# Fused four-layer residual kernel on one core: gathers placed behind a step's fourth maximum, three queries normed inside the attention loop, and smaller moves

## The chip, the core and the metric

The kernel runs on one core of a Trainium2 chip. The core has five engines that run their own instruction streams side by side: TensorE (PE, matrix products and transposes; its weight loads appear as PEld), VectorE (DVE), ScalarE (ACT), GpSimd (POOL) and SyncE (SP, which here only starts DMA transfers). The metric is the device time of one execution in microseconds, lower is better. The time of a kernel is the median of its runs.

## The reference

The input `x` is 64 sequences of 64 tokens with 512 features, float32. Four layers each add to it:

```
x = x + (x @ W[id] + b[id])                    # one of 16 experts for each sequence
x = x + (x @ W1.T + scaling * (x @ A.T) @ Bm.T)# one of 8 adapters of rank 16
x = x + attention(x)
x = x + (weights[subject] over the 64 tokens + bias[subject])   # one of 8 subjects
```

The attention has 8 query heads in 4 groups of keys and values, 64 wide. Queries and keys are normalised, multiplied by a gain and rotated by their position. The new keys and values are written into a paged cache of blocks of 16 positions, and each sequence then attends to the 256 positions up to each token:

```
q = rope(rms(q) * (1 + q_scale), pos)
k = rope(rms(k) * (1 + k_scale), pos)
k_blocks, v_blocks = cache with k, v written at pos
scores = q . k / 16, masked to pos - 256 < kpos <= pos
out = softmax(scores) . v @ Wo.T
```

## The kernel before

**Tiles and order.** The 4096 tokens are 32 tiles (`NT`) of 128, two sequences each. The order of instructions on every engine is the order in which the program writes them: a queue of its own for each engine, no reordering. The engines meet through semaphores. Scratch tiles come from pools; a tile's next use waits until the last reader of its buffer is done. PSUM has eight banks: seven in a ring that nearly all products share (`bank`, L99), and one, `py`, in a pool of its own (`pyp`).

**First part** (L185 to L784). The expert products (`layer0`, L275), their transposes (`turn0`, L298 and the addition at L299), and the adapter layer (`layer1`, L650 to L665) run over groups of 1, 1, 2 and then 4 tiles. Between them lie the transposes of the layer's result (`turn_x2`, L684), the product with the weights of keys and values and that with the weights of queries (`product`, L140, named `pk` and `pq`), and the normalisation and rotation of both (`turned`, L116 to L135). In `turned` ACT squares (L120), DVE sums (L122), ACT takes the root (L123), DVE forms the reciprocal (L126) and multiplies (L128), two more multiplications by half rows (L133) and one by a whole row (L134) rotate, and an addition on engine `X` (L135) ends it. Keys and values of all tiles go to `kvd` in memory (`keep_kv`), where old cache rows are copied as well (`copies`, L155 on POOL and L161 on SP). DVE also works out tables of addresses (`windows`, for example L498) and the sines and cosines (`rotation`). Near the start `warm` (L222) runs three and then six matmuls of the identity with itself, whose results nobody reads.

**Late queries.** With `LATE = 8`, the queries of tiles 25 to 31 are not made in the first part. Those of 25 to 30 are made in a loop ahead of the attention (L995 to L1003): product, `parts_q`, and two tiles later `turn_q` (L170), which transposes the query (`pqt`), lets ACT copy it twice and writes it to memory as `qTd`, from where `load_q` fetches it two steps before its use. Tile 31 has its product in step 0 of the loop, in the bank `py`; its normalisation runs in steps 0 to 3, so the bank is held until L128 of step 2 has read it. `turn_q` of tiles 29, 30 and 31 runs in steps 0, 4 and 5.

**Attention loop** (L1008 to L1046). Step `s` runs in this order:

1. `load_kv(s + 2)`: five gathers (L801) on POOL, by addresses that DVE worked out; masks, queries (SP).
2. `scores(s)`: eight products `ps` (L874); for each, DVE adds the mask and finds the maximum in one instruction (L882), ACT forms the exponential and its sum (L886).
3. POOL's addition to `w3` (`add_one`, L847); `load_pair`.
4. `attend(s - 1)`: 48 small matmuls `po` (L921, L934), then two copies to `oT` on DVE (L939).
5. `normalise(s)`: reciprocals and eight multiplications on DVE (L894, L898).
6. in even steps `last(s - 4)`: `pz` (L961), the fourth layer of two tiles.
7. `project(s - 2)`: `py` (L949) with the output weights, and an addition on DVE (L953).
8. `keys(s + 1)`: transposes `pkt` (L855, L861) and three ACT copies to `kT`.
9. `turn(s)`: transposes `ppt` of the normalised scores (L907, L911), copied to `pT` by DVE and ACT in turn (L908), the last by ACT (L912).

The buffers of gathered rows, `kv`, are four (L792). In steps 0 and 1 a POOL copy of one element of `kT` (`after_keys`, L809) stands ahead of the gathers; from step 2 on they only wait for a free `kv` buffer, that is for `po` of an earlier step.

Of the kernel before, what the change touches and what calls it, by code (L numbers as in the profile page):

```python
# [49 lines left out]
LATE = 8  # L50
# [9 lines left out]
def body(ctx: ExitStack, tc: tile.TileContext, a: dict, out: bass.AP):  # L60
# [55 lines left out]
    def turned(ps, n, to, pool, X, kind, cg, sg):  # L116
# [14 lines left out]
        for f in range(2):  # L131
            fs, of = slice(f * HALF, (f + 1) * HALF), slice((1 - f) * HALF, (2 - f) * HALF)
            V.tensor_tensor(t2[:, :, fs], qn[:, :, of], bc(sg[:, None, fs], [128, n, HALF]), ALU.mult)  # L133
        V.tensor_tensor(qn, qn, bc(cg[:, None, :], [128, n, HD]), ALU.mult)  # L134
# [8 lines left out]
    def parts_q(i, pq, X, cs=None):  # L143
        qr = late.tile([128, H, HD], F32, name="qr", bufs=2)
        qrs[i] = qr.rearrange("p h d -> p (h d)")
        return turned(pq, H, qr, late, X, 0, *(cs or gains(0, i, late, X)))
# [23 lines left out]
    def turn_q(i, pool=late):  # L170
# [4 lines left out]
        qT = pool.tile([128, 2, 2, 2, T], F32, name="qTs", bufs=2 if pool is late else 4)  # L175
# [9 lines left out]
    with ExitStack() as pa:  # L185
# [32 lines left out]
        def warm(n):  # L218

            pw = bank("pw")  # L220
            for _ in range(n):
                TE.matmul(pw[:, :128], ident, ident, start=True, stop=True)  # L222

        toki = ptok[:, : 4 * B].rearrange("p (k b) -> p k b", k=4)

        warm(3)
# [7 lines left out]
        warm(6)  # L234
# [497 lines left out]
        for g in range(NG - 1):  # L732
# [9 lines left out]
            for k in range(m):  # L742
# [13 lines left out]
                pk = product(i, wkv, "pk") if half else None  # L756
# [8 lines left out]
                if half == halves - 1:  # L765
                    keep_kv(i, pk if half else product(i, wkv, "pk"), P)
                    if i < NT - LATE:
                        asked.append(i)
                    if len(made) > 1:
                        turn_q(made.pop(0))  # L770
# [24 lines left out]
    kvs, kTs, mbs, prs, pTs, oTs, qTs, pairs, x3s = {}, {}, {}, {}, {}, {}, {}, {}, {}  # L795
# [10 lines left out]
    def after_keys(i):  # L806

        seen = bp.tile([1, 1], F32, name="seen")
        P.tensor_copy(seen, kTs[i][0:1, 0, 0:1])  # L809
# [54 lines left out]
    def scores(i):  # L864
        kT, mb, qT = kTs.pop(i), mbs.pop(i), qTs.pop(i)
        pr = bp.tile([128, G, 2 * NPOS], F32, name="pr")
        mx = bp.tile([128, G, 2], F32, name="mx")
        sm = bp.tile([128, G, 2], F32, name="sm")
        for gp in range(2):
            for b2 in range(2):  # L870
# [8 lines left out]
                for g2 in range(2):  # L879
# [4 lines left out]
                        op0=ALU.add, op1=ALU.min, accum_out=mx[:, g, b2 : b2 + 1],  # L884
                    )
                    S.activation(  # L886
                        p, p, AF.Exp, bias=mx[:, g, b2 : b2 + 1], scale=-1.0, accum_out=sm[:, g, b2 : b2 + 1],
# [26 lines left out]
    def attend(i):  # L914
# [19 lines left out]
        for gp in range(2):  # L934
            for b2 in range(2):
                for g in (2 * gp, 2 * gp + 1):
                    product(b2, g, slice(b2 * 64, (b2 + 1) * 64), 4, G, g, False, gp == 1)
        for b2 in range(2):
            V.tensor_copy(oT[:, :, b2, :], po[b2][:, :256].rearrange("p (k t) -> p k t", t=T))  # L939
# [49 lines left out]
    for i in range(2):  # L989
# [3 lines left out]

    parts = {}
    for i in range(NT - LATE + 1, NT - 1):  # L995
        pq = product(i, wq, "pq")
        parts[i] = parts_q(i, pq, V, cs[i])
# [5 lines left out]
        next(parts[i])  # L1003
    keys(0)
    load_q(1)
    load_mask(1)
    wo = bp.tile([128, KC, D], F32, name="wo", bufs=1)
    for s in range(NT):  # L1008
        if s + 2 < NT:
            if s < 2:  # L1010
                after_keys(s)
            load_kv(s + 2)
# [3 lines left out]
        scores(s)  # L1016
        if s >= 2:
            add_one(s - 2)
        if s:
            load_pair(s - 1)  # L1020
            attend(s - 1)
        else:

            parts[NT - 1] = parts_q(NT - 1, product(NT - 1, wq, "pq", pyp), V, cs[NT - 1])
            turn_q(NT - 3, bp)
        if s == 2:
            next(parts[NT - 1])
        normalise(s, 0)
        normalise(s, 1)
        if s % 2 == 0 and s >= 4:  # L1030
# [5 lines left out]
        if s in (4, 5):  # L1036
            turn_q(NT - 6 + s, bp)
        elif s in (2, 3):

            run(parts.pop(NT - 4 + s))  # L1040
# [4 lines left out]
        elif s == 1:  # L1045
            next(parts[NT - 1])  # L1046
# [5 lines left out]
    attend(i)  # L1052
# [57 lines left out]
```

## Time and profile before

| | us |
|---|---|
| median of 3 runs | 969.09 (968.87 to 969.17) |
| the profiled execution | 969.89 |
| its span | 967.9 |
| mean granted clock of PE in it | 0.993 |

The span is the time from the first to the last record of the profile; the profiled execution's own time lies 2.0 us above it. The attention loop begins with the first `ps` at 542.46 and takes the last 425 us.

The costliest groups of the lines that the change touches (columns: line, engine, operation, output and inputs, shape, count; busy us in all and mean ns of one; idle us of the engine just before them and what ended most of that):

```profile
L801 POOL DMA_INDIRECT kv<-kvd,idxn x128 | 126.5, 988 | 212.8 <-PE po L921 155.8
L886 ACT ACTIVATE pr<-pr,mx 128x320 f32<-128x320 f32 x256 | 140.1, 550 | 7.2 <-DVE mx L882 3.2
L882 DVE CUSTOM_DVE_ANT_0 pr<-ps,mb 128x320 f32<-128x320 f32 x256 | 107.8, 485 | 6.2 <-PE ps L874 4.4
L140 PE MATMUL pq<-wq,x 128*128 128x512 f32 x248 | 111.3, 593 | 0.0
L874 PE MATMUL ps<-kT,qT 64*128 64x320 f32 x512 | 87.3, 460 | 10.8 <-DVE pT L908 6.8
L908 DVE COPY pT<-ppt 128x512 f32<-128x512 f32 x64 | 41.9, 687 | 74.3 <-PE ppt L907 36.4
```

A float32 matmul shows as several records, so 256 products `ps` are 512 records. The gathers (L801) have a third of all of POOL's busy time, and 155.8 us of POOL's idle time before them ended with `po`, that is with the buffer coming free.

### The profile page before, as it was taken

To read this page: it belongs to the slowest core of one execution; us is meant where nothing else is said; L and a number is where in the kernel's file an instruction comes from. 1 tells how busy PE (TensorE), PEld (TensorE's weight loads), DVE (VectorE), ACT (ScalarE), POOL (GpSimd) and SP (SyncE) were. 2 spreads that over 40 slices of the span, in tenths; PEclk is the share of its full clock that TensorE was granted. 3 is DMA by queue.
4 is the path that set the end of the run, shared out by engine and by line. 5 is a ranking of instruction groups with operands and counts; after the bars stand their busy time and mean duration, and the time that the engine had idled before them with its cause. 6 is when DMAs were issued, how large, how long until landed. Compare 5 with 4: busy or idle time off the path is not lost.

```text
span 967.9 us, 17834 instructions
## 1 busy us (share of the span) xinstructions
PE 937.1 (97%) x5425; PEld 513.4 (53%) x5425; DVE 609.0 (63%) x1734; ACT 405.0 (42%) x1081; POOL 402.6 (42%) x604
## 2 busy tenths in 40 slices
PE   8989999999999999999899979999999999999998
PEld 4434444444444444443344546766666666666665
DVE  4744776866976476442216868666767776667673
ACT  1312122322223222233223656656666666666663
POOL 4234355554553544534425543334444333334400
PEclk9989999999999999999999989999999999999999
DMA  8888999999999999999954774766666565666621
GB/s 303 301 291 293 397 397 332 374 375 367 381 335 389 401 339 385 354 362 380 350 217 142 237 254 135 213 206 204 205 197 194 182 193 180 201 197 201 200 68 45
DMA packets 132944, 260.74 MB, mean 269 GB/s; under 512 B 32481, under 2 KB 41186, under 8 KB 132850
## 3 DMA queue, kind: packets, MB, share of 16 engines
q1 hardware_dynamic: 108722, 178.74, 51.3%
q0 software_dynamic: 23232, 79.71, 24.8%
q10 hardware_dynamic: 896, 1.16, 0.3%
q8 instruction: 43, 0.70, 0.3%
q14 instruction: 51, 0.42, 0.1%
HBM read 190.06 MB, written 69.50 MB: 268 GB/s over the span
## 4 chain that ended last, share of the span: by engine, by line
PE 90%; DMA 4%; DVE 3%; SPq 1%; issue 1%; ACT 1%; DVEq 0%; ACTq 0%
PE py L949 12%; PE p L665 11%; PE pq L140 11%; PE p L275 10%; PE pk L140 10%; PE po L921 8%; PE ps L874 8%; PE ppt L907 6%; DMA w<-in_W 3%; PE pkt L855 2%; PE ppt L911 2%; PE px L684 1%; PE pkt L861 1%; PE pqt L174 1%; PE pz L961 1%; PE pt L298 1%
## 5 line engine op out<-in xcount | busy, mean ns | idle before, releaser
L801 POOL DMA_INDIRECT kv<-kvd,idxn x128 | 126.5, 988 | 212.8 <-PE po L921 155.8
L886 ACT ACTIVATE pr<-pr,mx 128x320 f32<-128x320 f32 x256 | 140.1, 550 | 7.2 <-DVE mx L882 3.2
L275 PE MATMUL p<-w,xt 128*64 128x512 f32 x512 | 120.4, 601 | 2.7 <-DMA w<-in_W 2.7
L949 PE MATMUL py<-wo,oT 128*128 128x512 f32 (+1 forms) x264 | 118.3, 591 | 1.7 <-DVE qn L128 1.7
L155 POOL DMA_INDIRECT st<-in_kvc,cidx x68 | 65.9, 970 | 125.1 <-DMA kvd<-st 107.8
L140 PE MATMUL pk<-wkv,x 128*128 128x512 f32 x256 | 115.6, 596 | 0.6 <-ACT x L686 0.6
L665 PE MATMUL p<-w,x 128*128 128x512 f32 x256 | 114.4, 603 | 0.0
L882 DVE CUSTOM_DVE_ANT_0 pr<-ps,mb 128x320 f32<-128x320 f32 x256 | 107.8, 485 | 6.2 <-PE ps L874 4.4
L140 PE MATMUL pq<-wq,x 128*128 128x512 f32 x248 | 111.3, 593 | 0.0
L874 PE MATMUL ps<-kT,qT 64*128 64x320 f32 x512 | 87.3, 460 | 10.8 <-DVE pT L908 6.8
L908 DVE COPY pT<-ppt 128x512 f32<-128x512 f32 x64 | 41.9, 687 | 74.3 <-PE ppt L907 36.4
L133 DVE TENSOR_TENSOR sq<-qn,sg 128x256 f32<-128x256 f32 (+1 forms) x128 | 40.1, 354 | 75.4 <-POOL sg L110 73.5
L898 DVE TENSOR_SCALAR pr<-pr,sm 128x320 f32<-128x320 f32 x256 | 85.2, 394 | 2.2
L921 PE MATMUL po<-pT,kv 128*64 128x128 f32 (+1 forms) x1536 | 84.3, 281 | 1.3 <-issue 1.3
L921 PEld LDWEIGHTS po<-pT,kv 128*64 128x64 f32 (+1 forms) x1536 | 70.5, 137 | 22.0 <-DVE mx L882 14.0
L123 ACT ACTIVATE ss<-ss,epst 128x4 f32<-128x4 f32 (+1 forms) x64 | 19.1, 299 | 146.7 <-DVE ss L122 136.5
L949 PEld LDWEIGHTS py<-wo,oT 128*128 128x128 f32 x264 | 47.5, 189 | 61.5 <-issue 58.4
L665 PEld LDWEIGHTS p<-w,x 128*128 128x128 f32 x256 | 48.3, 193 | 59.0 <-issue 57.2
L140 PEld LDWEIGHTS pk<-wkv,x 128*128 128x128 f32 x256 | 46.3, 190 | 51.1 <-issue 49.8
L275 PEld LDWEIGHTS p<-w,xt 128*64 128x64 f32 x512 | 35.3, 137 | 71.5 <-issue 64.8
L135 POOL TENSOR_TENSOR qr<-qn,sq 128x512 f32<-128x512 f32 x25 | 31.8, 1273 | 90.2 <-DVE qn L134 60.8
L140 PEld LDWEIGHTS pq<-wq,x 128*128 128x128 f32 x248 | 44.9, 190 | 46.2 <-issue 46.2
(202 smaller groups left out, 1336.5 us busy)
## 6 DMA issues: line engine op xcount, KB each, us to landing
w<-in_W SPq DMA_DIRECT2D x62, 1024.0 KB
kvd<-st SPq DMA_DIRECT2D x68, 512.0 KB
xt<-in_xT SPq DMA_DIRECT2D x32, 256.0 KB
x2d<-x2n SPq DMA_DIRECT2D x32, 256.0 KB
kvd<-kvn SPq DMA_DIRECT2D x32, 256.0 KB
qTd<-qTs SPq DMA_DIRECT2D x32, 256.0 KB
qT<-qTd SPq DMA_DIRECT2D x32, 256.0 KB
x2r<-x2d SPq DMA_DIRECT2D x32, 256.0 KB
```

Of the source, the lines that this page charges most:

```text
L140: TE.matmul(ps, x2s[i][:, c, :], w[:, c, :], start=c == 0, stop=c == KC - 1)
L155: P.indirect_dma_start(out=st, out_offset=None, in_=a["kvc"].rearrange("(n r) d -> n (r d)", r=2), in_offset=bass.IndirectOffsetOnAxis(ap= ...
L275: TE.matmul(p0[hs, :], xs[i][:, c, hs], w0s[i][h][:, c, :], start=c == 0, stop=c == KC - 1)
L665: TE.matmul(p1[i], x1s[i][:, c, :], w1[:, c, :], start=c == 0, stop=False)
L801: P.indirect_dma_start(out=kv[:, n, :], out_offset=None, in_=kvd, in_offset=bass.IndirectOffsetOnAxis(ap=at, axis=0),)
L874: TE.matmul(ps[g2][:, :NPOS], qT[rows, gp, b2].rearrange("p h t -> p (h t)"), kT[rows, gp, b2 * NPOS : (b2 + 1) * NPOS], start=True, stop= ...
L882: V.tensor_tensor_reduce(out=p, in0=ps[g2][:, :NPOS], in1=mb[:, b2, :], scale=-1.0, scalar=3.0e38, op0=ALU.add, op1=ALU.min, accum_out=mx[ ...
L886: S.activation(p, p, AF.Exp, bias=mx[:, g, b2 : b2 + 1], scale=-1.0, accum_out=sm[:, g, b2 : b2 + 1],)
L898: V.tensor_scalar(p, p, sm[:, g, b2 : b2 + 1], None, ALU.mult)
L907: TE.transpose(pt[:, n * 128 : (n + 1) * 128], pr[:, g, at : at + 128], ident)
L921: TE.matmul(po[b2][g2 * 64 : (g2 + 1) * 64, gp * 128 : (gp + 1) * 128], kv[rows, n, (G + g) * HD : (G + g + 1) * HD], pT[rows, c, m * 128 ...
L949: TE.matmul(py[:, fs], oT[:, c].rearrange("p b t -> p (b t)"), wo[:, c, fs], start=c == 0, stop=c == KC - 1,)
```

## The change

It has six parts.

1. `warm` and its nine matmuls go.
2. In the first part the last `pk` of a group is written behind `turn0` instead of ahead of it, in groups whose tiles are handled by halves.
3. `turned` and `parts_q` take an engine `M` for the multiplications of the rotation; tile 28 has them, and the addition, on POOL. The buffers of `qTs` outside `late` go from four to three.
4. The tile of maxima, `mx`, becomes two, `mx0` for groups of heads 0 and 1 and `mx1` for 2 and 3. `after_keys` is replaced by `after_scores`: from step 1 on POOL copies one element that the fourth L882 of the step has written, and the five gathers of `load_kv(s + 2)` stand behind this copy, in all steps. Three `load_kv` instead of two run ahead of the loop.
5. `attend` ends without its two `oT` copies; they are `keep_outputs`, behind `normalise`.
6. The queries of tiles 29 to 31 (`LAST` on) are made in another way. The product is copied by ACT into an SBUF tile `raw` (29 ahead of the loop, 30 and 31 in steps 0 and 1 out of the bank `py`). POOL squares them in steps 2 to 4, DVE sums in steps 3 to 5, and in step 6 ACT takes one root for all three, with a one-column exponential behind it, and DVE one reciprocal. POOL multiplies and rotates in steps 7 to 12, two steps for each (`rotate_raw`), and `turn_q` runs in steps 9, 11 and 13. `turn_q` of tile 28 moves into step 1, that of 27 and `keys(0)` change places around the product of 29.

```diff
-    def turned(ps, n, to, pool, X, kind, cg, sg):
+    def turned(ps, n, to, pool, X, kind, cg, sg, M=V):
...
-            V.tensor_tensor(t2[:, :, fs], qn[:, :, of], bc(sg[:, None, fs], [128, n, HALF]), ALU.mult)
-        V.tensor_tensor(qn, qn, bc(cg[:, None, :], [128, n, HD]), ALU.mult)
+            M.tensor_tensor(t2[:, :, fs], qn[:, :, of], bc(sg[:, None, fs], [128, n, HALF]), ALU.mult)
+        M.tensor_tensor(qn, qn, bc(cg[:, None, :], [128, n, HD]), ALU.mult)
...
-        warm(3)
...
-        warm(6)
...
-                pk = product(i, wkv, "pk") if half else None
+                pk = product(i, wkv, "pk") if half and k < m - 1 else None
                 turn0(i0)
...
-                    keep_kv(i, pk if half else product(i, wkv, "pk"), P)
+                    keep_kv(i, pk if half and k < m - 1 else product(i, wkv, "pk"), P)
...
-    def after_keys(i):
+    def after_scores(i):
 
         seen = bp.tile([1, 1], F32, name="seen")
-        P.tensor_copy(seen, kTs[i][0:1, 0, 0:1])
+        P.tensor_copy(seen, mxs[i][0][0:1, 1, 1:2])
...
-        mx = bp.tile([128, G, 2], F32, name="mx")
+        mxs[i] = [bp.tile([128, 2, 2], F32, name=f"mx{gp}") for gp in range(2)]
...
+        return oT, po
+
+    def keep_outputs(oT, po):
         for b2 in range(2):
             V.tensor_copy(oT[:, :, b2, :], po[b2][:, :256].rearrange("p (k t) -> p k t", t=T))
...
-    for i in range(2):
+    for i in range(3):
         load_kv(i)
...
+    def keep_raw(i, pq):
+        S.copy(raw[:, i - LAST].rearrange("p h d -> p (h d)"), pq)
+
+    def rotate_raw(i, part):
+        x, t2, (cg, sg) = raw[:, i - LAST], sqr[:, (i - LAST) % 2], cs[i]
+        if part == 0:
+            P.tensor_tensor(x, x, bc(ssr[:, i - LAST, :, None], [128, H, HD]), ALU.mult)
+            for f in range(2):
+                fs, of = slice(f * HALF, (f + 1) * HALF), slice((1 - f) * HALF, (2 - f) * HALF)
+                P.tensor_tensor(t2[:, :, fs], x[:, :, of], bc(sg[:, None, fs], [128, H, HALF]), ALU.mult)
+        else:
+            P.tensor_tensor(x, x, bc(cg[:, None, :], [128, H, HD]), ALU.mult)
+            P.tensor_tensor(x, x, t2, ALU.add)
+            qrs[i] = x.rearrange("p h d -> p (h d)")
+
     parts = {}
-    for i in range(NT - LATE + 1, NT - 1):
-        pq = product(i, wq, "pq")
-        parts[i] = parts_q(i, pq, V, cs[i])
+    for i in range(NT - LATE + 1, LAST):
+        X = P if i == LAST - 1 else V
+        parts[i] = parts_q(i, product(i, wq, "pq"), X, cs[i], X)
...
+    run(parts.pop(LAST - 1))
     keys(0)
+    keep_raw(LAST, product(LAST, wq, "pq"))
+    turn_q(LAST - 2, bp)
...
     for s in range(NT):
         if s + 2 < NT:
-            if s < 2:
-                after_keys(s)
-            load_kv(s + 2)
             load_mask(s + 2)
...
         scores(s)
+        if s and s + 2 < NT:
+            after_scores(s)
+            load_kv(s + 2)
         if s >= 2:
             add_one(s - 2)
+        if 2 <= s <= 4:
+
+            x = raw[:, s - 2]
+            P.tensor_tensor(sqr[:, s % 2], x, x, ALU.mult)
+        elif 7 <= s <= 12:
+            rotate_raw(LAST + (s - 7) // 2, (s - 7) % 2)
         if s:
             load_pair(s - 1)
-            attend(s - 1)
-        else:
-
-            parts[NT - 1] = parts_q(NT - 1, product(NT - 1, wq, "pq", pyp), V, cs[NT - 1])
-            turn_q(NT - 3, bp)
-        if s == 2:
-            next(parts[NT - 1])
+            outs = attend(s - 1)
+        if s < 2:
+
+            keep_raw(LAST + 1 + s, product(LAST + 1 + s, wq, "pq", pyp))
+        elif s == 6:
+            S.activation(ssr, ssr, AF.Sqrt, bias=epst, scale=1.0 / HD)
+
+            S.activation(ssr1, ssr[:, 0, :1], AF.Exp, scale=-1.0)
         normalise(s, 0)
         normalise(s, 1)
+        if s:
+            keep_outputs(*outs)
+        if s == 6:
+            V.reciprocal(ssr, ssr)
...
-        if s in (4, 5):
-            turn_q(NT - 6 + s, bp)
-        elif s in (2, 3):
-
-            run(parts.pop(NT - 4 + s))
+        if s == 1:
+            turn_q(LAST - 1, bp)
+        elif s in (9, 11, 13):
+            turn_q(LAST + (s - 9) // 2, bp)
+        elif 3 <= s <= 5:
+
+            V.tensor_reduce(ssr[:, s - 3], sqr[:, (s - 3) % 2], AX.X, ALU.add)
         turn(s)
...
-    attend(i)
+    keep_outputs(*attend(i))
```

More of the change, by code (lines that the diff above doesn't have):

```diff
@@ L141, in product, with parts_q @@
         return ps
-    def parts_q(i, pq, X, cs=None):
+    def parts_q(i, pq, X, cs=None, M=V):
         qr = late.tile([128, H, HD], F32, name="qr", bufs=2)
         qrs[i] = qr.rearrange("p h d -> p (h d)")
-        return turned(pq, H, qr, late, X, 0, *(cs or gains(0, i, late, X)))
+        return turned(pq, H, qr, late, X, 0, *(cs or gains(0, i, late, X)), M)
     def copies(to, pool, ahead):
@@ L174, in turn_q @@
             TE.transpose(pqt[:, c * 128 : (c + 1) * 128], qrf[:, c * 128 : (c + 1) * 128], ident)
-        qT = pool.tile([128, 2, 2, 2, T], F32, name="qTs", bufs=2 if pool is late else 4)
+        qT = pool.tile([128, 2, 2, 2, T], F32, name="qTs", bufs=2 if pool is late else 3)
         for gp in range(2):
@@ L216, in body @@
             )
[L218 to L222, printed above, removed]
         toki = ptok[:, : 4 * B].rearrange("p (k b) -> p k b", k=4)
-        warm(3)
         takes = su.tile([E, B], F32, name="takes")
@@ L793, in body @@
     bp = ctx.enter_context(tc.tile_pool(name="bp", bufs=2))
-    kvs, kTs, mbs, prs, pTs, oTs, qTs, pairs, x3s = {}, {}, {}, {}, {}, {}, {}, {}, {}
+    kvs, kTs, mbs, prs, mxs, pTs, oTs, qTs, pairs, x3s = {}, {}, {}, {}, {}, {}, {}, {}, {}, {}
     def load_kv(i):
@@ L883, in scores @@
                         out=p, in0=ps[g2][:, :NPOS], in1=mb[:, b2, :], scale=-1.0, scalar=3.0e38,
-                        op0=ALU.add, op1=ALU.min, accum_out=mx[:, g, b2 : b2 + 1],
+                        op0=ALU.add, op1=ALU.min, accum_out=mxs[i][gp][:, g2, b2 : b2 + 1],
                     )
                     S.activation(
-                        p, p, AF.Exp, bias=mx[:, g, b2 : b2 + 1], scale=-1.0, accum_out=sm[:, g, b2 : b2 + 1],
+                        p, p, AF.Exp, bias=mxs[i][gp][:, g2, b2 : b2 + 1], scale=-1.0, accum_out=sm[:, g, b2 : b2 + 1],
                     )
@@ L992, in body @@
     load_mask(0)
+    LAST = NT - 3
+    raw = bp.tile([128, 3, H, HD], F32, name="raw", bufs=1)
+    sqr = bp.tile([128, 2, H, HD], F32, name="sqr", bufs=1)
+    ssr = bp.tile([128, 3, H], F32, name="ssr", bufs=1)
+    ssr1 = bp.tile([128, 1], F32, name="ssr1", bufs=1)
+    def keep_raw(i, pq):
[11 more added lines that the diff above has]
+            qrs[i] = x.rearrange("p h d -> p (h d)")
     parts = {}
-    for i in range(NT - LATE + 1, NT - 1):
-        pq = product(i, wq, "pq")
-        parts[i] = parts_q(i, pq, V, cs[i])
+    for i in range(NT - LATE + 1, LAST):
+        X = P if i == LAST - 1 else V
+        parts[i] = parts_q(i, product(i, wq, "pq"), X, cs[i], X)
         next(parts[i])
@@ L1044, in body @@
             nc.sync.dma_start(wo, a["woT"].rearrange("(c p) f -> p c f", p=128))
-        elif s == 1:
-            next(parts[NT - 1])
     i = NT - 1
```

## The prediction

> **What bounds the kernel now.** I read the page's busy times and chain first, then busy time by stretch, then the timeline where a stretch shows idle time on PE.
>
> ```profile
> PE 937.1 (97%) x5425; PEld 513.4 (53%) x5425; DVE 609.0 (63%) x1734; ACT 405.0 (42%) x1081; POOL 402.6 (42%) x604
> ...
> PE 90%; DMA 4%; DVE 3%; SPq 1%; issue 1%; ACT 1%; DVEq 0%; ACTq 0%
> ```
>
> PE is the path. The change moves PE's work and removes only nine small matmuls, so all it can win is time in which PE idles or runs slowly: 967.9 - 937.1 = 30.8 us of idle, and slow stretches. Busy time by stretch (second number: PE busy; PEclk is the granted clock):
>
> ```profile
> 52.00:62.65 10.65, 7.08 (x27) 3.66 (x26) 8.69 (x30) 1.05 (x3) 5.20 (x12) 0.68 1.01 366
> 530.00:580.00 50.00, 43.36 (x266) 26.89 (x265) 37.11 (x114) 30.63 (x84) 23.77 (x27) 0.93 0.77 247
> 580.00:930.00 350.00, 341.54 (x2909) 232.69 (x2909) 246.07 (x852) 219.26 (x630) 138.86 (x161) 1.00 0.60 189
> ```
>
> The change touches two of these: the start of the attention loop (530 to 580), and the steady loop, where 350 - 341.54 = 8.46 us are idle. PE in the start of the loop (start, duration, last bracket: idle before it and what ended it):
>
> ```profile
> 517.25 10.46 PE L140 MATMUL pq<-wq,x 128*128 128x512 f32 x24
> ...
> 542.46 3.25 PE L874 MATMUL ps<-kT,qT 64*128 64x320 f32 x16 [1.17 <-issue]
> ...
> 568.09 3.55 PE L874 MATMUL ps<-kT,qT 64*128 64x320 f32 x8 [2.12 <-ACT pT L908]
> 571.57 4.05 PE L921 MATMUL po<-pT,kv 128*64 128x128 f32 x48
> 577.29 3.70 PE L949 MATMUL py<-wo,oT 128*128 128x512 f32 x8 [1.68 <-DVE qn L128]
> ...
> 586.55 2.56 PE L921 MATMUL po<-pT,kv 128*64 128x128 f32 x48
> ```
>
> After 2.12 us of waiting, 48 matmuls of `po` take 4.05 us; in the next step they take 2.56 us. That is half clock: 50 us at 0.93 lack 3.5 us, so about 7 us ran at half. Now a steady step with gathers, and one near the end without:
>
> ```profile
> 824.33 1.91 PE L907 MATMUL ppt<-ident,pr 128*128 128x128 f32 x16
> 825.26 0.95 POOL L801 DMA_INDIRECT kv<-kvd,idxh  x1 [0.30 <-issue]
> 827.41 1.29 DVE L908 COPY pT<-ppt 128x512 f32<-128x512 f32 x2 [3.28 <-PE ps L874]
> 828.16 1.95 PE L874 MATMUL ps<-kT,qT 64*128 64x320 f32 x12 [0.74 <-DVE pT L908]
> ...
> 926.30 1.91 PE L907 MATMUL ppt<-ident,pr 128*128 128x128 f32 x16
> 926.94 0.69 DVE L908 COPY pT<-ppt 128x512 f32<-128x512 f32 x1 [0.84 <-PE ppt L907]
> ```
>
> Without gathers DVE copies the first transposed scores 0.64 us after PE starts them. With gathers it waits 3.08 us, though PE has long gone on. The copy starts 2.15 us after the step's fifth gather (825.26). In the other half of the steps, which hold `pz` and are 0.86 us longer, the fifth gather comes sooner (838.09, 0.07 us after `ppt` at 838.02) and the copy again starts 1.94 us after it (840.03). I read this so: PE's completions reach other engines late while GpSimd writes a gather, until about 2 us after the last one. In steps without `pz` it costs PE 0.74 us here, because `ps` waits for a bank that the copy frees.
>
> **The change part by part.**
>
> *Start of the loop.* PE's work from 517.25 to the first `py` of L949 at 577.29 is, at undisturbed rates: seven products of 3.44, five `pqt` of 0.44, three `pkt` of 1.09, two `ppt` of 2.19, three `ps` of 2.35, two `po` of 2.50: 24.1 + 2.2 + 3.3 + 4.4 + 7.1 + 5.0 = 46.1 us. It took 60.0, so 13.9 are lost: about 6.8 in idle gaps (1.17, 2.12, 1.68 and smaller), 3.5 by the clock, the rest in matmuls that start late. The causes: in step 2 ACT squares a query and loads two tables (3.5 us from 568.41), DVE reduces, and `py` waits until DVE has read the last query out of the single bank (1.68); and ten gathers from 551.77 to 566.3 lie over `ps`, `po` and `ppt`. The change takes the first two away (one ACT copy of 0.60 frees the bank), puts one product behind `ps` of step 1, and lets no gather start in step 1 before its fourth maximum. What it leaves: the softmax of step 0 is covered by one product and `pkt` only. From the start of `ps`: 1.1 us to a table load, 1.28 for it, eight exponentials of 0.545, 1.7 for half a normalisation make some 8.5 us, against 2.35 + 3.44 + 1.09 + half a `ppt`: 8.0; and now fifteen gathers instead of ten run in a row from 523.5 (1.25 us apart: to about 543), over `ps` of step 0 at about 537. Where gathers lay over `ps` (553 to 560) eight maxima took 6.3 us instead of 3.3. I charge 1.5 to 3 for this and 1 for late `kT` copies in step 1. Gain 13.9 - 3.4 = 10.5; bounds 4 (the clock halves once more, 3.5, and 3 more of waiting) and 13.9.
>
> *Gathers held.* Let P be the start of `ps`. Where DVE isn't held up (929.42 after 928.58) the fourth maximum is there at P + 2.4. The one-element copy takes 0.18, gathers followed it by 0.34 to 0.65 (551.43 to 551.77, 542.49 to 543.14), so they start at P + 2.9 to 3.2, the fifth 5.15 later at P + 8.2, and completions flow again at P + 10.2. `ppt` starts at P + 9.5 without `pz` and 10.4 with it; its first copy was due 0.64 later, P + 10.1. So the gap closes. What stands under the block now are `kT` copies: `pkt` ends from P + 8.8, ACT copies from 10.2 in three pieces (0.43, 0.43, 0.60) to 11.7, and the next `ps` at P + 11.8 wants the third by then. It fits, with 0.1 to 0.3 us of slack without `pz`, over 1 us with it. I take 7.0 of the 8.46; bounds 8.46 and -6 (all twelve or so steps without `pz` 1.2 us late instead of 0.7). The gathered rows are used about 12 us after the last gather instead of 22: hidden. POOL's queue behind the copy: five gathers (6.1), `w` (0.33), and in steps 2 to 4 and 7 to 12 up to 2.8 us of query work (1.27 for each 128x512, 0.73 for each half): 9.6 of at least 11.8 us a step. Without that slack each microsecond of it would delay the gathers.
>
> *Outputs behind the normalisation.* The two `oT` copies (0.76) come 3 us later on DVE. Their banks are wanted by `ppt` 5 us after `po`; DVE idled 0.65 before them and over 2 before `pT`. Nothing; 0.7 a step if that idle time were gone.
>
> *Last three queries.* DVE loses 3.7 us for each (0.69 five times, 0.20, 0.75 less one shared), POOL gains 6.5 for each (five of 1.27, less what two halves save). Three `pqt` move from prologue and steps 0, 4, 5 to 9, 11, 13; one more is left for later than before, 0.44, already within PE's total. Step 6 gets two table loads on ACT: rows at 569.04 and 570.66 show 1.28 each, with 0.30 between: 3.1 with a short exponential. ACT idled 2.69 before `kT` in such a step (837.51), and `kT` had 1 us to spare: nothing, at most 1.
>
> The Trainium skill ("ScalarE: Activation LUTs", What ACT_TABLE_LOAD costs) adds a drain of 1.38 us to each load. Here the root follows its load at once (570.34 after 569.04 + 1.28), so I see no drain; with it step 6 would lose another 2 us.
>
> *First part.* Nine warming matmuls go. They ran at the slow rate (0.22 us apart):
>
> ```profile
> 7.30 2.93 PE L222 MATMUL pw<-ident 128*128 128x128 f32 x12
> 10.16 4.27 PE L275 MATMUL p<-w,xt 128*64 128x512 f32 x16
> ```
>
> Transposes later go 0.11 apart (1.91 us for 16), and the 16 matmuls of 10.16 took 4.27 where 3.65 is usual: full speed came about 11.5. Without them PE idles from about 6 to 10.16. Bounds: nothing (full speed comes as before), and 3.4 (half speed for the 6.8 us that both slow stretches above lasted). I take 2.0, as PE was slow for 5.2 us after it resumed at 57.44 and lost 2.6. Behind it PE has one hole, 0.34 at 36.69, until 53.9, so 1.7 arrives. The moved `pk` wins nothing at 57.44: there PE waits 3.56 us for DVE's row of L498, whose order is the same.
>
> The rule of the skill ("TensorE: Matmul & The Clock Gate", What's actually happening) is that one busy window of 3.4 us lifts the gate, and an idle one lowers it. Rows here show 6.8 us, twice the window. By the rule the loss would be about 1.2 instead of 2.0, and the sum 0.8 lower.
>
> Sum: -10.5 - 7.0 + 1.7 + 0.5 (step 6, reductions before `pT` in steps 3 to 5) = -15.3. The profiled execution took 969.89 (span 967.9 and 2.0 around it): 954.6. It is 0.8 above the median, so 953.8 against 969.09.
>
> **The rivals.**
> 1. *Fifteen gathers spoil the start.* For: maxima slowed to 6.3 us under gathers; PE halves its clock after some 2 us of idleness. Against: one product and `pkt` need no maximum. The gain there is 4: -4 - 7 + 2.2 = -8.8, 960.3.
> 2. *The hold does nothing*, since the late copies come from something else than gathers. For: PE's ends are modelled. Against: 1.9 to 2.2 us after the fifth gather in both kinds of step, and on time without gathers. Steady gain 0: -8.3, 960.8.
> 3. *The held gathers stop the next step (slower).* If completions flow at P + 12 instead of 10.2, `kT` is done at 13.5 and `ps` waits 1.7 us in each of 13 steps without `pz` and 0.8 in 13 with it: 32.5 - 8.5 = +24, with the rest +15.5: 984.6. It decides from P + 11.5 on, where new waits reach 17 us. For: the slack of 0.1 to 0.3. Against: POOL is idle 2 us a step, so only slower gathers could do it.
>
> **How the numbers follow.** My forecast 58%, rival 1 16%, rival 2 10%, rival 3 12%, no change 4%. This kernel's measurement can tell 0.2% (1.9 us) from no change. Faster: 58 + 16 + 10 = 84%; slower 12%. The forecast's own range is 947 (gains 13.9 and 8.46, loss 0.5) to 958; up to 964 it takes in rivals 1 and 2 with 3 us of margin.
>
> **What would show it.** Right: from 530 to 580 clock 1.00 and PE idle under 4 us; `pT` copies 0.7 to 1.1 us after `ppt` in every step; steady idle time under 3 us; the first gather 2.9 to 3.2 us after `ps`. Wrong: `ps` waiting for ACT's `kT`; PE idle over 2 us in step 0 with half clock after it; a first part longer by over 4 us, or not longer.

## The result, and the profile after

| | before | changed |
|---|---|---|
| median, us | 968.98 (968.81 to 969.17) | 980.14 (978.1 to 983.59) |
| profiled execution / its span | 969.89 / 967.9 | 978.1 / 976.3 |
| ratio to before | | 1.0111 (1.0085 to 1.0138) |

The changed kernel is slower by 1.1%; 1.6% faster was predicted. First the busy times and the chain of waits of the changed kernel, then its busy time in the two stretches of the prediction (second number: PE busy).

```profile
PE 936.0 (96%) x5407; PEld 514.4 (53%) x5407; DVE 602.5 (62%) x1713; ACT 400.8 (41%) x1080; POOL 427.4 (44%) x653
...
PE 67%; DMA 3%; issue 2%; ACT 1%; DVE 1%; SPq 1%; POOL 0%; ACTq 0%; POOLq 0%; DVEq 0%
```

```profile
530.00:580.00 50.00, 44.39 (x293) 29.12 (x293) 29.26 (x97) 28.49 (x81) 24.10 (x27) 0.93 0.70 214
580.00:930.00 350.00, 334.39 (x2835) 229.51 (x2832) 242.03 (x832) 213.64 (x625) 159.41 (x202) 1.00 0.63 188
```

PE has the same work (936.0 against 937.1) in a longer span. In the steady loop it idles 15.6 us of 350, where it was 8.46, and the start of the loop runs at a mean clock of 0.93 as before. By the starts of `ps` of each step, the span is 8.4 us longer by these parts:

| stretch | before | changed | difference | predicted |
|---|---|---|---|---|
| up to the `pq` products ahead of the loop (517.25, 515.50) | 517.25 | 515.50 | -1.75 | +1.7 |
| from there to `ps` of step 3 | 66.95 | 64.09 | -2.9 | -10.5 |
| steps 3 to 30 | 357.0 | 370.0 | +13.0 | -6.5 |
| from step 31 on | 26.7 | 26.7 | 0 | 0 |

The steady loop loses 13.0 us, and what lies ahead of it wins 4.6. The waits in the steady loop have moved. These groups are of the kernel before (last columns: idle time of the engine just before these instructions, and what ended it), then of the changed one:

```profile
L908 ACT COPY pT<-ppt 128x512 f32<-128x512 f32 x64 | 34.9, 591 | 49.1 <-PE ps L874 21.3 <-PE ppt L907 15.9 <-PE ppt L911 12.0
L939 DVE COPY oT<-po 128x256 f32<-128x256 f32 x64 | 24.2, 419 | 24.8 <-PE po L921 24.8
```

```profile
L900 DVE COPY pT<-ppt 128x512 f32<-128x512 f32 x64 | 42.4, 684 | 6.3 <-PE ppt L899 6.1
L900 ACT COPY pT<-ppt 128x512 f32<-128x512 f32 x64 | 35.9, 622 | 6.0 <-PE ppt L899 5.8
L934 DVE COPY oT<-po 128x256 f32<-128x256 f32 x64 | 24.9, 420 | 81.0 <-PE pkt L853 31.2 <-PE pkt L847 22.2 <-remote 19.1
```

The wait ahead of the `pT` copies is gone, on ACT from 49.1 us to 6.0 and on DVE from 74.3 (shown with the profile before) to 6.3. The wait ahead of the `oT` copies has grown from 24.8 to 81.0 in its place. One step of the changed kernel, without `pz`; P, the start of its `ps`, is 765.54 (timeline: start, duration, last bracket idle before it):

```profile
765.54 2.63 PE L866 MATMUL ps<-kT,qT 64*128 64x320 f32 x16
768.10 2.56 PE L913 MATMUL po<-pT,kv 128*64 128x128 f32 x48
...
768.35 0.18 POOL L801 COPY seen<-mx 1x1 f32<-1x1 f32 x1 [5.82 <-DVE mx L874]
...
769.07 0.99 POOL L793 DMA_INDIRECT kv<-kvd,idxn  x1 [0.54 <-issue]
...
771.36 0.18 ACT L878 ACTIVATION_READ_ACCUMULATOR pr<-pr,mx 128x1 f32 x1
...
771.58 0.18 DVE L886 RECIPROCAL sm<-sm 128x4 f32<-128x4 f32 x1
...
771.79 1.27 DVE L890 TENSOR_SCALAR pr<-pr,sm 128x320 f32<-128x320 f32 x4
...
774.14 0.82 PE L847 MATMUL pkt<-ident,kv 128*128 128x128 f32 x6
774.19 0.95 POOL L793 DMA_INDIRECT kv<-kvd,idxh  x1 [0.30 <-issue]
775.04 0.38 PE L853 MATMUL pkt<-ident,kv 128*128 128x128 f32 x2
...
776.47 0.38 PE L853 MATMUL pkt<-ident,kv 128*128 128x128 f32 x2 [1.05 <-issue]
776.60 0.76 DVE L934 COPY oT<-po 128x256 f32<-128x256 f32 x2 [3.53 <-remote]
...
776.91 0.86 ACT L848 COPY kT<-pkt 128x384 f32<-128x384 f32 x2 [5.36 <-PE pkt L853]
```

`po` ends at P + 5.1 and the normalisation at P + 7.5. The two copies of `po` start only at P + 11.1, 2.4 us after the fifth gather began, and ACT's copy of `kT` 0.3 us after them. ACT's ends are not late in this time: DVE's reciprocal (771.58) starts 0.04 us after ACT has read the last sum. PE too stands still, from 775.42 to 776.47, and goes on just when the others do. What it does there (the last two of the four matmuls of L853, in the bank that the first two wrote) needs nothing that isn't long there, and the view names no releaser ("issue").

### The profile page after: what moved, and what is told of

The parts are those of the page before. It is cut to its first block, busy times and chain, and to the rows that moved or that the text cites. A ratio compares the mean times of both kernels' runs of the same rounds, so it can differ in the third digit from the quotient of the medians.

```text
span 976.3 us, 17740 instructions
## 1 busy us (share of the span) xinstructions
PE 936.0 (96%) x5407; PEld 514.4 (53%) x5407; DVE 602.5 (62%) x1713; ACT 400.8 (41%) x1080; POOL 427.4 (44%) x653
## 4 chain that ended last, share of the span: by engine, by line
PE 67%; DMA 3%; issue 2%; ACT 1%; DVE 1%; SPq 1%; POOL 0%; ACTq 0%; POOLq 0%; DVEq 0%
PE py L944 12%; PE ps L866 8%; PE po L913 8%; PE pk L140 6%; PE p L657 6%; PE ppt L899 6%; PE pq L140 5%; PE p L267 4%; PE pkt L847 2%; PE pkt L853 2%; DMA kvd<-st 1%; PE ppt L903 1%; PE pz L956 1%; DMA w<-in_W 1%; PE pqt L174 1%
## 5 line engine op out<-in xcount | busy, mean ns | idle before, releaser
L140 PE MATMUL pq<-wq,x 128*128 128x512 f32 x240 | 107.7, 593 | 0.0
L890 DVE TENSOR_SCALAR pr<-pr,sm 128x320 f32<-128x320 f32 x256 | 87.4, 403 | 2.3
L866 PE MATMUL ps<-kT,qT 64*128 64x320 f32 x512 | 82.7, 447 | 4.1 <-issue 2.2
L913 PE MATMUL po<-pT,kv 128*64 128x128 f32 (+1 forms) x1536 | 82.1, 278 | 0.0
L944 PEld LDWEIGHTS py<-wo,oT 128*128 128x128 f32 x264 | 47.5, 189 | 61.1 <-issue 59.9
L133 DVE TENSOR_TENSOR sq<-qn,sg 128x128 f32<-128x128 f32 (+1 forms) x120 | 37.0, 350 | 69.0 <-POOL sg L110 67.2
L913 PEld LDWEIGHTS po<-pT,kv 128*64 128x64 f32 (+1 forms) x1536 | 68.8, 135 | 19.8 <-DVE mx L874 13.6
L801 POOL COPY seen<-mx 1x1 f32<-1x1 f32 x29 | 5.2, 178 | 162.4 <-DVE mx L874 162.4
L934 DVE COPY oT<-po 128x256 f32<-128x256 f32 x64 | 24.9, 420 | 81.0 <-PE pkt L853 31.2
```

Of the source, the lines that this page charges most:

```text
L140: TE.matmul(ps, x2s[i][:, c, :], w[:, c, :], start=c == 0, stop=c == KC - 1)
L866: TE.matmul(ps[g2][:, :NPOS], qT[rows, gp, b2].rearrange("p h t -> p (h t)"), kT[rows, gp, b2 * NPOS : (b2 + 1) * NPOS], start=True, stop= ...
L890: V.tensor_scalar(p, p, sm[:, g, b2 : b2 + 1], None, ALU.mult)
L913: TE.matmul(po[b2][g2 * 64 : (g2 + 1) * 64, gp * 128 : (gp + 1) * 128], kv[rows, n, (G + g) * HD : (G + g + 1) * HD], pT[rows, c, m * 128 ...
L944: TE.matmul(py[:, fs], oT[:, c].rearrange("p b t -> p (b t)"), wo[:, c, fs], start=c == 0, stop=c == KC - 1,)
```

## The experiments

P is the start of a step's first `ps`; all times by step come from the traces.

**First set, against the changed kernel: the order of the outputs, the hold, the gathers.**

The first puts the outputs ahead of the normalisation:

```diff
-            outs = attend(s - 1)
+            keep_outputs(*attend(s - 1))
...
-        if s:
-            keep_outputs(*outs)
```

The second and third take the hold away and put `load_kv` at the head of the step again, as before the change. The third, shown here, has two loads ahead of the loop; the second keeps three, so its `load_kv` and `after_keys` (the copy of one element of `kT`) begin in step 1:

```diff
-    for i in range(3):
+    for i in range(2):
         load_kv(i)
...
         if s + 2 < NT:
+            if s < 2:
+                after_keys(s)
+            load_kv(s + 2)
             load_mask(s + 2)
...
-        if s and s + 2 < NT:
-            after_scores(s)
-            load_kv(s + 2)
```

The fourth leaves the gathers of the loop out and uses the rows of tiles 0 to 2 again:

```diff
     for i in range(3):
         load_kv(i)
+    kvs0 = dict(kvs)
...
             after_scores(s)
-            load_kv(s + 2)
+            kvs[s + 2] = kvs0[(s + 2) % 3]
```

> The changed kernel with one thing undone: the two oT copies stand ahead of the normalisation again; the gathers stay behind the fourth maximum. Theory (PE's completions reach other engines late from the first gather of a step until some 2.2 us after its fifth starts, so the oT copies start at P + 11 although po ends at P + 5): now DVE stands at the first oT copy until P + 11 and the normalisation is queued behind it, so ppt starts at P + 13 to 15 instead of 9.5 to 11; a step takes 16 us instead of 13.2, and the whole some 1060 us (1040 to 1100). Rival (the hold is harmless, and what costs is that the oT copies stand behind eight multiplications): the copies start at P + 5 as in the kernel before, steps fall to 12.3, and the time to 955 to 962.

> The changed kernel with the hold undone: load_kv(s + 2) stands at the head of step s again and waits only for its buffer (in step 1 behind a copy of one element of kT); three load_kv stay ahead of the loop, and the oT copies stay behind the normalisation. Theory: the gathers start only when po's completion has arrived (P + 5.3 to 6.2), so the oT copies find it and start at P + 8 with the normalisation's end; steps 3 to 31 take 357 us as before the change instead of 370, and the time is 967 (964 to 970). Rival (the order of the outputs costs): steps stay at 13 us, 976 to 982. Rival (the query work on POOL costs): steps 3 to 12 stay long.

> As the run without the hold, and with two load_kv ahead of the loop and those of steps 0 and 1 behind a copy of one element of kT, all as before the change. Theory: step 0 loses its three waits of PE (2.16, 1.39 and 0.57 us) and the half clock behind them in part, as ten gathers instead of fifteen lie ahead of it; 3 us less than with three ahead, 964 (961 to 967). Rival (step 0 waits because only one product and pkt cover its softmax, whatever the gathers do): within 1 us of the run with three ahead.

> The changed kernel without the gathers of the loop: steps 3 to 31 read the rows of tiles 0 to 2 again, so this leaves out 145 of the 160 gathers; all else is unchanged, the copy behind the fourth maximum too. Theory: with no gather PE's completions arrive at once, oT copies start with the end of the normalisation at P + 7.7, steps take 11.8 and 12.6 us, steps 3 to 31 some 355 us instead of 370, the time 965 (962 to 968), with step 0 as long as before (18 us). Rival (PE waits for the oT copies because of DVE's own work, or for POOL's query work): steps of 13 us stay, 976 to 982.

Measured, beside 948.36 of the kernel before: 946.60 (ratio 0.9976, 0.9958 to 0.9994), 944.65 (0.9966, 0.9951 to 0.9981), 939.40 (0.9904, 0.9869 to 0.9939), 943.10 (0.9938, 0.9915 to 0.9961). None of my numbers for the four fits, because this chip isn't like the first one: the kernel before takes 948 on it and not 969, and in all four traces steps 3 to 30 take 342.5 to 342.7 us, with the gathers in any place or left out. So the runs told nothing of the hold; the one thing that they told is that ten gathers instead of fifteen ahead of step 0 save 3.9 us in steps 0 to 2 (33.2 against 37.1).

**The two kernels on such a chip.**

> The changed kernel itself once more, beside the kernel before, since the four runs above met a chip on which the kernel before takes 948 us instead of 969 and on which no step waits for completions with any place of the gathers. Theory (whether GpSimd's gathers hold back PE's completions differs from chip to chip, and the change is slower only where they do): where the kernel before takes 948, the changed kernel's oT copies start at P + 7.7, its steps take 11.8 and 12.6 us, and its time is 943 to 946; where the kernel before takes 969, they start at P + 11 and it takes 978 to 984. Rival (the outputs behind the normalisation together with the hold cost by themselves, on any chip): slower than the kernel before by some 10 us on this chip too.

> The kernel before, for its trace on the same chip. Theory: where it takes 948, no gap in ps after steps without pz (0.74 us on the first chip), steps of 11.8 and 12.6; where it takes 969, the gaps as in the profile before. Rival (the 21 us between the chips lie elsewhere, in the first part or at the start of the loop): the gaps are there at 948 too.

Measured: changed 944.63 against 948.30, ratio 0.9963 (0.9941 to 0.9986), and the kernel before 948.08 in its profiled run. Here the change makes the kernel faster. Steps 3 to 30 take 342.0 us before and 342.7 after, without any gap, so it gains nothing there; in the two profiles the time from the last transposition of `turn_x2` to the first `ps` falls from 40.3 to 35.7. One step of the changed kernel here, P = 743.01:

```profile
745.37 2.56 PE L913 MATMUL po<-pT,kv 128*64 128x128 f32 x48
745.82 0.18 POOL L801 COPY seen<-mx 1x1 f32<-1x1 f32 x1 [5.38 <-DVE mx L874]
746.54 0.99 POOL L793 DMA_INDIRECT kv<-kvd,idxn  x1 [0.54 <-issue]
...
750.68 0.74 DVE L934 COPY oT<-po 128x256 f32<-128x256 f32 x2
...
751.59 0.94 POOL L793 DMA_INDIRECT kv<-kvd,idxh  x1 [0.30 <-issue]
...
753.13 0.69 DVE L900 COPY pT<-ppt 128x512 f32<-128x512 f32 x1 [0.84 <-PE ppt L899]
```

The gathers are made at the same places (P + 3.5 to P + 8.6) and last as long, but DVE takes `po` at P + 7.7, in the middle of them. That a gather holds back what PE has finished is thus not a property of the kernel: of the seven chips of these experiments three show it (the kernel before at 970 to 975), as the chip of the first profiles did, and four don't (947 to 949). Each was met in one set of runs only, so whether it lasts in a chip or is a state that passes can't be told.

**The same on a chip that holds back.**

Three kernels of the first set, and one with transfers by SP. These read whole blocks of rows, so the addressing is left out; the one-element copy goes into the buffer, so that they wait for the same maximum:

```diff
+    def load_rows(s):
+        i = s + 2
+        kv = kvs[i] = kvp.tile([128, 5, 2 * G * HD], F32, name="kv")
+        P.tensor_copy(kv[0:1, :, 0:1], mxs[s][0][0:1, 1, 1:2][:, None, :].to_broadcast([1, 5, 1]))
+        for n in range(5):
+            r = OLD + (2 * i + n) % NT * 128
+            nc.sync.dma_start(kv[:, n, :], kvd[r : r + 128, :])
...
-            after_scores(s)
-            load_kv(s + 2)
+            load_rows(s)
```

> The oT copies ahead of the normalisation, the hold kept, once more, to meet a chip of the first kind (the kernel before at 969). There the theory of late completions expects DVE to stand at the oT copy until P + 11 and the normalisation behind it: steps of 16 us, some 1060 us. Rival (late completions come only from the order in which DVE reads): 955 to 962. Where the kernel before takes 948, both expect 944 to 948.

> No hold, two load_kv ahead of the loop, as the run of that name. On a chip where the kernel before takes 969, theory: steps 3 to 31 as before the change (357 us instead of 370), 964 (960 to 967), faster than both kernels there; rival (not the hold but the outputs behind the normalisation): 976 or more. Where the kernel before takes 948: 939 to 942 again, faster than both.

> The changed kernel with the 145 gathers of the loop replaced by transfers of the same size that SP starts, behind a one-element POOL copy at the same place (fourth maximum). They read whole blocks of rows instead of the addressed ones, so the addressing is left out. Theory (the holding back of completions comes from GpSimd's making of the gathers, not from 640 rows being moved): on a chip with the kernel before at 969, oT copies start at P + 7.7, steps of 11.8 and 12.6, 964 or less. Rival (the moved data hold them back): steps of 13 us stay, some 978. Where the kernel before takes 948: no wait in any step, as with gathers.

> Without the gathers of the loop, once more, 145 of 160 left out. On a chip with the kernel before at 969: theory, steps 3 to 31 take some 355 us instead of 370, the time 962 to 966; rival (the waits come from DVE's or POOL's own work): 976 to 982. Where the kernel before takes 948: 941 to 944.

Beside 970.61 of the kernel before: 1025.64 (one run), 966.07 (0.9953, 0.9933 to 0.9973), 949.10 (one run), 954.84 (one run). By stretch:

| | steps 0 to 2 | steps 3 to 30 |
|---|---|---|
| before (first chip) | 41.7 | 357.0 |
| changed (first chip) | 44.0 | 370.0 |
| outputs ahead of the normalisation | 47.4 | 414.4 |
| no hold, two ahead | 43.4 | 356.9 |
| no gathers in the loop | 41.8 | 342.7 |
| transfers by SP instead | 42.1 | 342.7 |

Without gathers in the loop no step from 1 on waits, on this chip as on the others. Nor does one with the same number of bytes moved behind the same maximum by SP (P = 749.85):

```profile
752.21 2.56 PE L921 MATMUL po<-pT,kv 128*64 128x128 f32 x48
...
752.85 2.23 SPq L795 DMA_DIRECT2D kv<-kvd  x5
...
757.29 0.75 DVE L942 COPY oT<-po 128x256 f32<-128x256 f32 x2
```

So it is the gathers that GpSimd makes and not the amount moved. What of them it is was not tested apart: SP's transfers are started within 2.2 us instead of 6.1 and without addresses. Without the hold the steady loop takes 356.9, as before the change (the two loads ahead instead of three alter only the first steps). This run keeps the new order of the outputs and the query work on GpSimd, so neither is what costs. With the outputs ahead of the normalisation one step (P = 793.47) reads:

```profile
796.02 2.56 PE L913 MATMUL po<-pT,kv 128*64 128x128 f32 x48
...
796.99 0.99 POOL L793 DMA_INDIRECT kv<-kvd,idxn  x1 [0.54 <-issue]
...
802.04 0.95 POOL L793 DMA_INDIRECT kv<-kvd,idxh  x1 [0.30 <-issue]
...
804.48 0.76 DVE L934 COPY oT<-po 128x256 f32<-128x256 f32 x2 [6.70 <-PE pkt L853]
805.36 1.27 DVE L890 TENSOR_SCALAR pr<-pr,sm 128x320 f32<-128x320 f32 x4
805.80 1.32 PE L899 MATMUL ppt<-ident,pr 128*128 128x128 f32 x8 [2.48 <-DVE pr L890]
```

DVE stands for 6.70 us at a copy of what PE had finished at P + 5.1; it starts 2.4 us after the fifth gather, and the normalisation and `ppt` come after it. I had 1040 to 1100 for this; it is 1026, since in some steps the end of `po` slips through between two gathers (copies at P + 7.0 to 8.4), and these take 13 us instead of 16. Not all of the time is waiting: the granted clock from 580 to 990 is 0.95 in the mean, where it is 1.00 in the changed kernel, and 0.05 of 410 us is some 20 us (an estimate) of the 44 by which steps 3 to 30 exceed those of the changed kernel. Without the hold, P = 763.38:

```profile
768.66 0.99 POOL L793 DMA_INDIRECT kv<-kvd,idxn  x1 [6.30 <-PE po L917]
...
770.97 0.73 DVE L938 COPY oT<-po 128x256 f32<-128x256 f32 x2
...
773.71 0.95 POOL L793 DMA_INDIRECT kv<-kvd,idxh  x1 [0.30 <-issue]
...
775.90 1.29 DVE L904 COPY pT<-ppt 128x512 f32<-128x512 f32 x2 [3.21 <-PE ppt L907]
776.64 0.54 PE L870 MATMUL ps<-kT,qT 64*128 64x320 f32 x2 [0.67 <-DVE pT L904]
```

The first gather here waits for the end of `po` itself, so `oT` finds it delivered and follows the normalisation at P + 7.6; what is late again are the `pT` copies, for 0.67 us of PE.

**The start of the loop, and the hold at the eighth maximum.**

In the first and third, two loads stand ahead of the loop, tile 2's gathers behind the fourth maximum of step 0, tile 3's behind the eighth of step 1, in the third also tile 4's behind the eighth of step 2, and there is no hold after that (shown for the third):

```diff
-        P.tensor_copy(seen, mxs[i][0][0:1, 1, 1:2])
+        P.tensor_copy(seen, mxs[i][min(i, 1)][0:1, 1, 1:2])
...
         if s + 2 < NT:
+            if s > 2:
+                load_kv(s + 2)
...
-        if s and s + 2 < NT:
+        if s < 3:
             after_scores(s)
             load_kv(s + 2)
```

The second is the changed kernel with its hold at the eighth maximum, the fourth the changed kernel:

```diff
-        P.tensor_copy(seen, mxs[i][0][0:1, 1, 1:2])
+        P.tensor_copy(seen, mxs[i][1][0:1, 1, 1:2])
```

> From step 2 on no hold, as in the run with two load_kv ahead of the loop; the gathers of tile 2 stand behind the fourth maximum of step 0, those of tile 3 behind the eighth maximum of step 1, so that in these two steps none lies over ps. On a chip with the kernel before at 970, theory: step 0 takes 9 to 11 us and step 1 12 to 14 instead of 9.5 and 21.8, the time 956 to 960. Rival (step 0 or 1 waits for its softmax whatever the gathers do): 964 to 967 as without this. Where the kernel before takes 948: 938 to 942.

> The changed kernel with the gathers behind the eighth maximum instead of the fourth. On a chip with the kernel before at 970, theory (what counts is which of PE's ends lie under the gathers): they start at P + 5.0, just behind po's end at P + 4.9, so most oT copies start at P + 7.7 again and steps 3 to 31 take 357 to 361 us instead of 370, the time 966 to 972. Rival (any hold costs, or the outputs behind the normalisation do): 977 to 984. Where the kernel before takes 948: 943 to 947, nothing told apart.

> As the run with the gathers of tiles 2 and 3 placed, and those of tile 4 behind the eighth maximum of step 2 too, since there they followed at once and lay over ps of step 2 (17.5 us); no hold from step 3 on. On a chip with the kernel before at 970 or more, theory: steps 0 to 2 together take 35 to 38 us instead of 43.8, the time 960 to 963. Rival (the loss only moves one step on): step 3 or 4 takes 16 to 17 us, 966 to 969. Where the kernel before takes 948: 938 to 942.

> The changed kernel on the same chip, for a direct comparison. Theory: where the kernel before takes 969 or more, 1.0085 to 1.0138 of it, with oT copies at P + 11; where it takes 948, 0.994 to 0.999 of it. Rival (the first result was one chip's accident): not slower on a chip with the kernel before at 969 or more.

The first two expected, beside 973.77: 968.29 (0.9956, 0.9937 to 0.9975) and 972.33 (0.9986, 0.9959 to 1.0013). The other two, on another chip, beside 974.95: 967.02 (0.9923, 0.9906 to 0.9939) and 985.23 (1.0111, 1.0094 to 1.0127).

| | step 0 | step 1 | step 2 | step 3 | steps 3 to 30 |
|---|---|---|---|---|---|
| changed (last set) | 18.5 | 15.0 | 13.4 | 12.9 | 373.3 |
| no hold, two ahead | 9.5 | 21.8 | 12.1 | 12.8 | 356.9 |
| tiles 2 and 3 placed | 10.5 | 15.8 | 17.5 | 13.0 | 359.2 |
| tiles 2, 3 and 4 placed | 10.1 | 13.3 | 13.6 | 14.6 | 361.1 |
| eighth maximum, three ahead | 17.8 | 12.2 | 13.7 | 12.0 | 362.8 |

The change's 1.0111 is found again to the fourth digit. The first and fourth row are of one chip, the third and fifth of another, the second is of the set above. Where gathers lie over `ps`, that step takes 17.5 to 21.8 us (step 0 of the first row, step 1 of the second, step 2 of the third); placed behind the maxima they cost 1 to 2, and steps 0 to 2 fall to 36.9 as expected. The rival was right in small: step 3, where two bursts now meet, takes 14.6 instead of 12.8 to 13.0 without such a meeting. That does not explain why the median is 967 and not 960 to 963, since the profiled run, which has this step, took 960.79; the other four took 966.8 to 971.3 and have no trace. With the hold at the eighth maximum the copies of `oT` start at P + 7.3 to 8.8, about as expected, and steps 3 to 30 take 362.8, a little more than my 357 to 361: a hold there wins nothing over none (359.2 on the same chip).

**The hold at the second and at the third maximum.** Two `load_kv` ahead, the hold in every step; each was run on two chips.

```diff
-        P.tensor_copy(seen, mxs[i][0][0:1, 1, 1:2])
+        P.tensor_copy(seen, mxs[i][0][0:1, 1, 0:1])
```

```diff
-        P.tensor_copy(seen, mxs[i][0][0:1, 1, 1:2])
+        P.tensor_copy(seen, mxs[i][0][0:1, 0, 1:2])
```

> The hold moved from the fourth to the second maximum of a step, in every step from 0 on, and two load_kv ahead of the loop instead of three. On a chip with the kernel before at 969 or more, theory (PE stops at P + 9.7 when the gathers have held back its ends until P + 10.9; a block that ends 0.8 us sooner reaches no stop and no copy that is due): first gather at P + 2.7, fifth at P + 7.8, ends delivered at P + 10.1, steps 3 to 30 together 345 to 352 us instead of 370 (342.7 without gathers, 357 without a hold), steps 0 to 2 some 36, the time 950 to 957. Rival (gathers so early hold back the last products ps, whose ends come at P + 2.5, and so the maxima): steps of 14 us and more, over 985. Where the kernel before takes 948: 938 to 942.

> The same with the third maximum: first gather at P + 3.1, fifth at P + 8.2, ends delivered at P + 10.5. Theory: between the second and the fourth, steps 3 to 30 together 352 to 362 us, the time 958 to 966 on a chip with the kernel before at 969 or more. Rival (the place within the maxima doesn't matter, any hold ahead of po's end costs 13 us): 370 us, 972 to 976. Where the kernel before takes 948: 938 to 942.

> The hold at the second maximum once more, to meet a chip of the first kind. With the kernel before at 969 or more, theory: ends delivered at P + 10.1, steps 3 to 30 together 345 to 352 us, the time 950 to 957. Rival (gathers so early hold back the last ps and so the maxima): steps of 14 us and more, over 985. Where the kernel before takes 948: 942 again, nothing told apart.

> The hold at the third maximum once more. With the kernel before at 969 or more, theory: 352 to 362 us for steps 3 to 30, the time 958 to 966. Rival (any hold ahead of po's end costs 13 us): 370 us, 972 to 976. Where the kernel before takes 948: 942 again.

Inconclusive: both times the kernel before took 947 to 949. There they took 942.08 and 942.07, then 942.77 and 942.80 (ratios 0.993 to 0.994 in all four), steps 0 to 2 33.2 us and steps 3 to 30 342.7. What they do where gathers hold back is not known.

## Why the prediction was wrong, step by step

**Gathers held: -7.0 predicted, +13.0 found; this is the step that failed.** What it said of the gathers was right in kind: PE's ends reach the others only some 2 us after the last gather, the hold moves this time, and the `pT` copies no longer wait (in many steps because `ppt` itself is late). Two things were wrong. The block was put at P + 2.9 to P + 10.2 and is at P + 3.5 to P + 10.9: the copy of one element runs at P + 2.8, as the maximum is that late, the first gather starts 0.72 us behind it instead of 0.34 to 0.65, and the ends flow 2.3 us after the fifth gather, not 2.0. And "what stands under the block now are `kT` copies" left out what the block had never covered before: the end of `po` itself. Before, the first gather waited for that end, as it waits for the buffer, so it was always delivered ahead of the block. Behind the fourth maximum the gathers start 1.5 us before `po` ends. Two runs, on other chips than the first, bear this out: without the hold steps 3 to 30 take 356.9 instead of 370.0, and with the hold so late that the gathers start at P + 5.0 or after, about when `po` ends, 362.8.

How it reaches PE I can only say in part. The `oT` copies come at P + 11 instead of P + 7.6. In steps without `pz` the third `ppt` is the first product in a bank of `po`, in steps with `pz` the first `ppt` is. Without `pz` the third was due at about P + 10.4 (`ppt` started at 9.5 before the change), and the copy that frees its bank ends at about P + 11.4: by these rows the bank alone would cost some 1 us in such a step (an estimate). But in most steps PE has stopped before that, at P + 9.5 to 10.9, in `pkt` and the first `ppt`, which need neither `oT` nor a bank that isn't free. Behind each stop 8 to 12 of PE's ends arrive within some 0.5 us from P + 10.7 to 11.2 on; in the kernel before there were at most 7, and no such stop (steps 14 to 23 of both). Their number alone does not decide it: in steps 16 and 20 of the changed kernel 11 arrive in the same way, and PE stops for no more than 0.15 us. What stops it stays open.

**Outputs behind the normalisation: costed at nothing, and nothing it is.** Without the hold that order leaves the steady loop at 356.9 against 357.0. With the hold it saves much: 414.4 with the old order against 370.0 (each pair is of two chips).

**Start of the loop: -10.5 predicted, -2.9 found.** Rival 1 had the mechanism: fifteen gathers reach over `ps` of step 0. PE in that step of the changed kernel, and the last of the fifteen:

```profile
535.54 1.88 PE L866 MATMUL ps<-kT,qT 64*128 64x320 f32 x10
539.58 0.80 PE L866 MATMUL ps<-kT,qT 64*128 64x320 f32 x2 [2.16 <-issue]
...
540.40 0.95 POOL L793 DMA_INDIRECT kv<-kvd,idxh  x1 [0.31 <-issue]
...
541.77 1.43 PE L866 MATMUL ps<-kT,qT 64*128 64x320 f32 x2 [1.39 <-ACT qTs L177]
543.78 1.43 PE L866 MATMUL ps<-kT,qT 64*128 64x320 f32 x2 [0.57 <-DVE mx L874]
545.14 5.14 PE L140 MATMUL py<-wq,x 128*128 128x512 f32 x8
```

Eight products need 9.6 us instead of 2.35, and behind the pauses the clock halves (granted clock 0.50 from 541.3 to 548.0; 1.43 for two records against 0.80, 5.14 for a product instead of 3.70). I charged 1.5 to 3 us for it; step 0 took 18.0, and 11.5 on a chip that doesn't hold back. With ten gathers ahead it took 9.5 on a chip that does. The waits of step 2 did go, those for the bank and for the table loads: it took 19.75 us before and takes 13.58 after.

**Idle time as the bound of a gain.** I took 8.46 us of idle PE as all that the steady loop could win. Without gathers steps 3 to 30 take 342.7 instead of 357.0, that is 14.3 less, and the kernel before itself takes 342.0 on a chip that doesn't hold back: matmuls that start late stand in the profile as busy ones.

**First part: +1.7 predicted.** The warming matmuls were themselves in the way. PE in the changed kernel:

```profile
6.46 3.68 PE L267 MATMUL p<-w,xt 128*64 128x512 f32 x8 [0.24 <-DMA w<-in_W]
10.51 2.75 PE L267 MATMUL p<-w,xt 128*64 128x512 f32 x8 [0.36 <-DMA w<-in_W]
...
16.77 1.06 PE L642 MATMUL pxa<-x,ao 128*32 128x128 f32 x8 [2.07 <-DMA ao<-in_aT]
```

The first half of the weights is there at 6.46, when the kernel before still had warming matmuls to run until 10.16. Half of the product runs at the slow rate in time that was lost anyway, and it ends at 13.3 instead of 14.4. I had taken this time for idle. But the gain of 1.1 us is gone at 16.77, where PE now waits for the transfer of `ao`; before, this product started at 16.72. The 1.75 us at 515.50 have another source: 0.5 is there by 56.95, and 1.1 more comes from a stretch at half clock that lasted 3.4 us instead of 6.8 (granted clock 0.50 from 56.6 to 59.9, before from 55.9 to 62.6). Other runs with the changed first part show either length there (3.4 us with tiles 2 and 3 placed, 6.8 with the hold at the eighth maximum), so that much of the gain is luck. What arrives at the end of the first part can't be told: the last transposition of `turn_x2` starts at 502.1 and 502.7 in two profiles of the kernel before, and at 498.5 to 506.3 in eighteen with the changed first part.

**Rival 3** had the right side with the wrong victim: it let `ps` wait for `kT` and put the point of decision at P + 11.5. At P + 10.9 `kT` was late by 2 us but not waited for, and the loss was there already. (Its sum in the prediction is 0.2 short: 24 - 8.3 is 15.7.) Rival 2 fell: the late copies do come from the gathers, as they vanish with them.

## What to carry to other kernels

Before moving a transfer that slows other engines, list every result that will now finish while it runs, and not only those that the move frees: here the old place was safe because the gather waited for the very end that it would have held back. Ask also whether the slowing is the kernel's or the chip's: where gathers hold nothing back the same change is 0.4% faster (0.9963). The version with no hold and two loads ahead beats the kernel before on both kinds of chips (0.9904 and 0.9953); the changed kernel, on other chips of these kinds, had 0.9963 and 1.0111. Where gathers hold back, placing the loads of the first three steps as well gave 0.9923, again on another chip.

## What the runs showed of the hardware that was not expected

- On some chips PE's completions were held back while GpSimd made gathers, until about 2.3 us after the last one began (970 us for the kernel before), on others not at all (948 us). Which it is stayed the same within every set of runs; why chips differ is not known. The same number of bytes moved by SP held nothing back (342.7 us for steps 3 to 30, as without gathers).
- In that time PE ran on by itself for some 5 us after the end of `po`, then in most steps stopped, for up to 1.2 us at a time, with nothing open that it needed as far as the trace tells.
- Taking away nine warming matmuls cost nothing that could be measured: the first product ended at 13.3 instead of 14.4 us.
